# A local transformer's layers: softmax over whole PSUM banks, feed-forward parts and norm rows moved in the step

## The chip, the core and the metric

One core of a Trainium2 chip runs one launch. The metric is device time in microseconds. The core has a matmul engine (PE, with its weight loads shown as PEld), a vector engine (DVE), an activation engine (ACT), GpSimd (POOL), and SyncE (SP), which issues the DMAs. The engines take their instructions in program order, each from its own queue, and wait for each other by semaphores. [...]

## What is computed

The kernel runs two modulated layers over 16 sequences of 256 tokens and 128 channels. The change lies in the feed-forward part of the first, which is itself a local transformer of six layers (16 heads of 64, windows of 32 tokens):

```python
def attn_layer(x, Wqkv, qs, ksc, Wo):
    q, k, v = heads of x @ Wqkv
    q = l2norm(q) * qs
    k = l2norm(k) * ksc
    q = q * cos * scale + rotate_half(q) * sin * scale
    k = k * cos / scale + rotate_half(k) * sin / scale
    # each window of 32 queries sees its own 32 keys and the 32 before them
    sim = einsum('bhwie,bhwje->bhwij', bq, bk2) * 8
    sim = where(mask, -max, sim)
    attn = softmax(sim, -1)
    return heads joined (attn @ bv2) @ Wo

def ffn_layer(x, g, bln, W1, b1, W2, b2):
    mu = x.mean(-1); var = ((x - mu) ** 2).mean(-1)
    xn = (x - mu) / sqrt(var + 1e-05) * g + bln
    a, gate = split(xn @ W1 + b1)
    return a * gelu(gate) @ W2 + b2

for i in range(6):
    x = attn_layer(shift_tokens(x), ...) + x
    x = ffn_layer(shift_tokens(x), ...) + x
```

The output is (16, 256, 128), all in float32.

## The kernel before

Before the six layers stands a linear-attention stage, after them a multi-query attention stage; the change touches neither. The six layers run as one loop of steps `n` (line 1050), with the order on PE, DVE, ACT and POOL written out by hand: each engine runs its instructions in the order in which the program issues them.

A unit `u` is two sequences side by side, 512 columns; there are eight units and eight head pairs, and a step works on two head pairs of one unit, `m = 2n` and `2n + 1`. So a unit takes four steps, a layer 32, all six 192. A step is a software pipeline: it projects the head pairs of step n, adds the rotated halves for n - 1, fetches norm factors for n - 3, does scores and softmax for n - 4, flips the probabilities of n - 5, and so on. In program order a step issues:

- `scaled` (POOL): two products of keys with their norm factors `kn`, 128x512 each (line 795).
- `merging` (PE): 16 heads of the weighted state through the merged output weights into the `y` bank; at the end of a unit (n mod 4 = 0) `add_to_state` (DVE).
- in odd steps `norms_rows`: PE transposes the factors `rk`, ACT copies them, SP writes them to DRAM.
- place A: `go_on(behind)` lets the feed-forward of a finished unit, a generator, go on by one part; then the merging of the next layer's weights.
- `rotate` (POOL): four additions of the halves that came back by DMA (`got`).
- `flipped` for x = 0: four PE transposes of the probabilities `pr` and a copy to `prT` on ACT; then in odd steps `windows` (eight PE transposes, copies on ACT and DVE, a DMA); `masked`, which puts the mask into two `sim` banks by a bf16 matmul; `flipped` for x = 1, its copy on DVE.
- in even steps `norms_sum` (PE, 8 matmuls, a copy on ACT).
- `weighted`: 8 matmuls, and four copies to `zx` on ACT and DVE. Then place B.
- `scores`: 64 small matmuls into the two `sim` banks (par = 0 and 1, eight rows of 64 keys each). `maxima` (DVE): a maximum over keys for each bank, then `nb`, its product with the norm factors of the queries.
- in even steps `norms_inverse`: PE transposes, two DVE instructions (`nx`, `ny`), then 13 small POOL instructions, three rounds of an inverse square root. Then place C.
- `project`, twice (with place D after the first): for q and k a matmul, a square on ACT, two products on DVE; then four DMAs that swap halves (`got <- sent`). Between them `exponentials` is fed in, two at a time: 16 activations of 128x64, each with its own bias, scale and accumulated sum, `pr` straight from the `sim` banks.
- `divided`, once for each x: a reciprocal on DVE, and a product on POOL (line 880).
- `widened`: SP fetches `kn` from DRAM, four DMAs.

PSUM is divided into four rotating banks (`mm`), three for `sim` and one for `y`. An `mm` bank is written again when whoever read it four allocations before is done.

The feed-forward, appended to `behind` ahead of place C of a step with n mod 4 = 0, takes these places before the change: mean and its subtraction in C, the square in D; in the next step (n mod 4 = 1) variance, `rs` and `ex` (POOL, lines 972 and 974) in A, the transposes `rb` with the normalisation and the affine (line 981, DVE) in C; the gates with their GELU in A of the step after (2), `pa` in A of step 3, `py` in A of the next step 0.

Of the kernel before, what the change touches and what calls it, by code (L numbers as in the profile page):

```python
# [44 lines left out]
def adaln_kernel(  # L45
# [554 lines left out]
    with ExitStack() as es:  # L600
# [196 lines left out]
        def windows(u, s):  # L797


            xw = atile("xw", (128, 8, 128))  # L800
            for g in range(2):
                pt = bank()
                for j in range(4):
                    w0 = 32 * (4 * g + j)
                    nc.tensor.transpose(  # L805
                        pt[0:64, j * 128 : (j + 1) * 128], zs[u][:, s, w0 : w0 + 64], ident
                    )
                dst = xw[0:64, 4 * g : 4 * g + 4, :].rearrange("p w d -> p (w d)")
                if g:
                    nc.vector.tensor_copy(dst, pt[0:64, :])  # L810
                else:
                    nc.scalar.copy(dst, pt[0:64, :])
            nc.sync.dma_start(xw[64:128], xw[0:64])
            return xw
# [37 lines left out]
        def maxima(sim, rn):  # L852

            mx = small("mx", (128, 8))
            nc.vector.tensor_reduce(mx, sim.rearrange("p (b k) -> p b k", b=8), AX.X, ALU.max)  # L855
            nb = small("nb", (128, 8))
            nc.vector.scalar_tensor_tensor(nb, mx, -1.0, rn, ALU.mult, ALU.mult)  # L857
            return nb

        def exponentials(x, sims, nbs, rn, pr, ssum):  # L860

            for par in range(2):
                for st in range(4):
                    b = 4 * x + st
                    nc.scalar.activation(  # L865
                        pr[:, x, st, par, :],
                        sims[par][:, b * 64 : (b + 1) * 64],
                        AF.Exp,
                        bias=nbs[par][:, b : b + 1],
                        scale=rn[:, par, b : b + 1],  # L870
                        accum_out=ssum[:, x, st, par : par + 1],
                    )
                    if st % 2:
                        yield

        def divided(pr, ssum):
            rsum = small("rsum", (128, 8))
            nc.vector.reciprocal(rsum, ssum.rearrange("p t h -> p (t h)"))  # L878
            prf = pr.rearrange("p t h k -> p (t h) k")
            nc.gpsimd.tensor_tensor(  # L880
                prf, prf, rsum.unsqueeze(2).to_broadcast([128, 8, 64]), ALU.mult
            )

        def flipped(p, x, pr, prT):

            pt = bank()
            for st in range(4):
                nc.tensor.transpose(  # L888
                    pt[:, st * 128 : (st + 1) * 128],
                    pr[:, x, st].rearrange("p h k -> p (h k)"),  # L890
                    ident,
                )
            if x:
                nc.vector.tensor_copy(prT[:, p + x, :], pt)
            else:
                nc.scalar.copy(prT[:, p + x, :], pt)
# [51 lines left out]
        def ffn(u, i):  # L948
# [10 lines left out]
            yield  # L959
            pv = bank()  # L960
# [15 lines left out]
            yield  # L976
# [4 lines left out]
            nc.vector.tensor_scalar(xn, xn, bcol(i, "g"), bcol(i, "b"), ALU.mult, ALU.add)  # L981
            yield
            yield
# [9 lines left out]
            yield  # L993
            yield
            yield
            yield
# [9 lines left out]
            yield  # L1006
            yield
            yield
            yield
# [40 lines left out]
        while n < N + 9 or behind:  # L1050
# [26 lines left out]
            for s, lag in ((0, 7), (1, 9)):  # L1077
                v, r = divmod(n - lag, QS)
                if r == 0 and 0 <= v < DEPTH * NU:
                    xws[v, s] = windows(v % NU, s)  # L1080
            sims = masked() if 0 <= n - 4 < N else None
            if 0 <= n - 5 < N:
                flipped(p, 1, prs.pop(n - 5), prTs[i, u])

# [3 lines left out]
            if 0 <= v < DEPTH * NU:  # L1088
                zxs[v, r] = weighted(r, xws[v, r // 2], prTs[v // NU, v % NU])
            go_on(behind)  # L1090
            if sims:
# [4 lines left out]
                nbs = [maxima(sims[par], rn[:, par]) for par in range(2)]  # L1096
                ssum = small("ssum", (128, 2, 4, 2))
# [13 lines left out]
            if sims:  # L1111
                for x in range(2):
                    for _ in between:
                        pass
                    divided(pr[:, x], ssum[:, x])
                    between = exponentials(1, sims, nbs, rn, pr, ssum) if x == 0 else iter(())
# [481 lines left out]
```

## Time and profile before

| what | us |
|---|---|
| three runs: median (lowest to highest) | 4207.4 (4207.33 to 4213.38) |
| the profiled execution | 4207.77 |
| its span, first to last instruction | 4206.0 |
| first scores (line 843) to last ones in it | 303.0 to 3571.9 |
| busy in the span: PE, DVE, ACT, POOL | 3938.9, 2856.0, 2753.1, 2655.1 |

| row (line, engine, what) | count | mean ns |
|---|---|---|
| 865 ACT, one exponential of 128x64 | 3072 | 454 |
| 865 ACT, reading its accumulator | 3072 | 255 |
| 855 DVE, maximum of a bank | 384 | 685 |
| 857 DVE, `nb` 128x8 | 384 | 412 |
| 878 DVE, reciprocal 128x8 | 384 | 197 |
| 880 POOL, division of 128x512 | 384 | 1042 |
| 714 POOL, rotation, two full inputs | 768 | 1272 and 1292 |
| 795 POOL, keys times their factors | 384 | 1274 |
| 894 DVE and 896 ACT, copy to `prT` | 192 and 192 | 691 and 585 |
| 810 DVE and 812 ACT, copy of windows | 96 and 96 | 683 and 578 |
| 981 DVE, affine of the feed-forward | 48 | 835 |

Durations overlap where an engine starts the next instruction before the last one is out: eight exponentials in a row start 0.38 us apart although a row says 454 ns and each has a read of its accumulator behind it. In what follows a line of the timeline gives the start, the duration, the engine, the source line, the operation, output and inputs, the shapes, and in brackets how long the engine had been idle and what ended it. A line of the waits gives the engine, the line that waited, what it waited for, the sum in us, how often, and the longest.

### The profile page before, as it was taken

Reading aid. Unit: us, or ns where it says so; the run is one execution under the profiler, and the core shown is the slowest. Engines: PE = TensorE matmul, PEld = TensorE weight load, DVE = VectorE, ACT = ScalarE, POOL = GpSimd, SP = SyncE. Lnnn points to the kernel's source line nnn. Section 1 sums busy time; section 2 is a strip of 40 time slices with the busy share of each in tenths; the row PEclk is TensorE's granted clock in tenths of the full one; section 3 lists DMA queues with packets and bytes.
Section 4 is the critical chain, followed back from the end, with each engine's and each line's share of the span. In section 5 each row is a group of like instructions: output and inputs, shape, how many; then the busy total and the mean of one; then the engine's idle time right before and its main releaser. Section 6 shows DMA issues by size and latency. Waiting matters only on the chain.

```text
span 4206.0 us, 118202 instructions
## 1 busy us (share of the span) xinstructions
PE 3938.9 (94%) x45491; PEld 2580.1 (61%) x45491; DVE 2856.0 (68%) x6005; ACT 2753.1 (65%) x9640; POOL 2655.1 (63%) x3374
## 2 busy tenths in 40 slices
PE   7877999999999999999999999999999999799998
PEld 4534666666666666666666666666666666455554
DVE  6746767677767767676777777776767675476664
ACT  4535666667666666667666667666666766276665
POOL 5446666776666676666676766767666665155453
PEclk9878999999999999999999999999999999899999
DMA  1333444444444444444444444444434442200000
GB/s 41 41 90 97 106 109 105 109 107 105 106 105 114 104 110 105 105 110 102 111 109 105 112 103 106 108 110 105 110 100 105 104 105 72 64 1 6 9 3 11
DMA packets 193547, 371.06 MB, mean 88 GB/s; under 512 B 42537, under 2 KB 83416, under 8 KB 192984
## 3 DMA queue, kind: packets, MB, share of 16 engines
q1 hardware_dynamic: 192984, 363.50, 34.3%
q8 instruction: 360, 5.90, 0.6%
q14 instruction: 203, 1.66, 0.1%
HBM read 127.92 MB, written 8.91 MB: 33 GB/s over the span
## 4 chain that ended last, share of the span: by engine, by line
PE 46%; DVE 22%; ACT 19%; issue 7%; POOL 5%; DMA 1%; SPq 0%; POOLq 0%; DVEq 0%; ACTq 0%
ACT pr L865 11%; PE mm L906 9%; PE sim L843 7%; DVE sent L703 6%; ACT sq L701 4%; PE mm L722 4%; PE mm L888 4%; POOL pr L880 4%; DVE k L706 3%; DVE q L706 3%; PE mm L698 3%; DVE mx L855 3%; PE mm L805 2%; PE mm L1376 2%; PE sim L1303 2%
## 5 line engine op out<-in xcount | busy, mean ns | idle before, releaser
L865 ACT ACTIVATE pr<-sim,nb,rq 128x64 f32<-128x64 f32 x3072 | 1229.5, 454 | 336.8 <-DVE nb L857 318.3
L880 POOL TENSOR_TENSOR pr<-pr,rsum 128x512 f32<-128x512 f32 x384 | 398.3, 1042 | 807.3 <-DVE rsum L878 761.8
L865 ACT ACTIVATION_READ_ACCUMULATOR pr<-sim,nb,rq 128x1 f32 x3072 | 784.5, 255 | 0.0
L927 PEld LDWEIGHTS y<-zx,wvo 128*128 128x128 f32 x6144 | 716.1, 192 | 92.1 <-issue 89.0
L927 PE MATMUL y<-zx,wvo 128*128 128x128 f32 x6144 | 717.7, 275 | 1.3 <-ACT zx L921 1.2
L698 PE MATMUL mm<-z,wqk 128*128 128x512 f32 x1536 | 706.9, 602 | 8.6 <-DMA wqk<-in_L_ffn_Wqkv_dram 6.7
L703 DVE SCALAR_TENSOR_TENSOR sent<-mm,vec,rope 128x512 f32<-128x512 f32 x768 | 570.4, 743 | 118.2 <-ACT sq L701 110.2
L714 POOL TENSOR_TENSOR q<-q,got 128x512 f32<-128x512 f32 x384 | 488.3, 1272 | 12.7 <-DMA got<-sent 10.2
L714 POOL TENSOR_TENSOR k<-k,got 128x512 f32<-128x512 f32 x384 | 496.2, 1292 | 0.0
L795 POOL TENSOR_TENSOR k<-k,kn 128x512 f32<-128x512 f32 x384 | 481.9, 1274 | 17.9 <-DMA kn<-rkh 17.9
L701 ACT ACTIVATE sq<-mm 128x512 f32<-128x512 f32 x768 | 475.7, 619 | 23.3 <-PE mm L698 23.3
L698 PEld LDWEIGHTS mm<-z,wqk 128*128 128x128 f32 x1536 | 278.7, 192 | 322.9 <-issue 234.7
L919 DVE COPY zx<-mm 128x512 f32<-128x512 f32 x384 | 265.6, 692 | 262.0 <-PE mm L906 262.0
L921 ACT COPY zx<-mm 128x512 f32<-128x512 f32 x384 | 224.9, 586 | 287.0 <-PE mm L906 287.0
L906 PE MATMUL mm<-prT,xw 64*128 64x256 f32 x3072 | 389.7, 391 | 3.8 <-DVE zx L919 2.0
L855 DVE TENSOR_REDUCE mx<-sim 128x8 f32<-128x512 f32 x384 | 263.1, 685 | 171.9 <-PE sim L843 171.9
L906 PEld LDWEIGHTS mm<-prT,xw 64*128 64x128 f32 x3072 | 293.5, 187 | 121.7 <-issue 92.2
L1346 POOL TENSOR_TENSOR pr<-pr,rsum 128x256 f32<-128x256 f32 (+1 forms) x256 | 205.1, 832 | 241.7 <-DVE rsum L1344 218.3
L888 PE MATMUL mm<-ident,pr 128*128 128x128 f32 x1536 | 244.6, 282 | 105.1 <-POOL pr L880 75.9
L888 PEld LDWEIGHTS mm<-ident,pr 128*128 128x128 f32 x1536 | 174.9, 142 | 270.0 <-POOL pr L880 240.6
L843 PEld LDWEIGHTS sim<-k,q 64*32 64x32 f32 x24576 | 265.8, 105 | 83.3 <-issue 55.2
L843 PE MATMUL sim<-k,q 64*32 64x64 f32 x24576 | 299.7, 226 | 15.9 <-POOL k L795 8.1
(253 smaller groups left out, 6461.5 us busy)
## 6 DMA issues: line engine op xcount, KB each, us to landing
got<-sent SPq DMA_DIRECT2D x1536, 128.0 KB
kn<-rkh SPq DMA_DIRECT2D x768, 128.0 KB
xw<-xw SPq DMA_DIRECT2D x96, 256.0 KB
wqk<-in_L_ffn_Wqkv_dram SPq DMA_DIRECT2D x48, 128.0 KB
bhome<-brow SPq DMA_DIRECT2D x1, 3072.0 KB
wv<-in_L_ffn_Wqkv_dram SPq DMA_DIRECT2D x12, 256.0 KB
wo<-in_L_ffn_Wo_dram SPq DMA_DIRECT2D x12, 256.0 KB
xt<-in_x_dram SPq DMA_DIRECT2D x8, 256.0 KB
```

The source lines that it names most:

```text
L698: nc.tensor.matmul(pp, wqk[:, j, :], xs, start=True, stop=True)
L701: nc.scalar.activation(sq, pp, AF.Square)
L703: nc.vector.scalar_tensor_tensor(two(sent[:, j, :]), two(pp), scale, tab[1], ALU.mult, ALU.mult)
L714: nc.gpsimd.tensor_tensor(r, r, two(got[:, j, :]), ALU.add)
L795: nc.gpsimd.tensor_tensor(k, k, two(kn), ALU.mult)
L843: nc.tensor.matmul(sims[par][32 * c : 32 * c + 32, c0 : c0 + 64], q[r, s, t0 : t0 + 32], k[r, s, t0 : t0 + 64], start=False, stop=True, sk ...
L855: nc.vector.tensor_reduce(mx, sim.rearrange("p (b k) -> p b k", b=8), AX.X, ALU.max)
L865: nc.scalar.activation(pr[:, x, st, par, :], sims[par][:, b * 64 : (b + 1) * 64], AF.Exp, bias=nbs[par][:, b : b + 1], scale=rn[:, par, b ...
L880: nc.gpsimd.tensor_tensor(prf, prf, rsum.unsqueeze(2).to_broadcast([128, 8, 64]), ALU.mult)
L888: nc.tensor.transpose(pt[:, st * 128 : (st + 1) * 128], pr[:, x, st].rearrange("p h k -> p (h k)"), ident,)
L906: nc.tensor.matmul(pz[par][:, w * 256 : (w + 1) * 256], xw[r, (2 * k + w) % 8, :], prT[r, :, 64 * k + 32 * w : 64 * k + 32 * w + 32], star ...
L927: nc.tensor.matmul(py[:, j * 128 : (j + 1) * 128], vo[:, h, :], zx[:, h % 2, h // 2, :], start=(h == 0), stop=(h == 2 * NP - 1), skip_grou ...
```

## The change

The softmax is done a bank at a time. Instead of the maxima times the norm factors as a bias, and 16 activations with sums of their own, DVE subtracts the maximum from a bank of scores (into `pr`), POOL multiplies by the norm factor of the query, ACT takes one exponential over the bank, in place, DVE adds up over keys, and after one reciprocal POOL divides. The order of the generator puts exponentials, sums, reciprocal and both divisions behind the matmul of the third projection (q of the second head pair), that is ahead of the third and fourth squares on ACT and the last four products on DVE.

```diff
-        def maxima(sim, rn):
-            mx = small("mx", (128, 8))
-            nc.vector.tensor_reduce(mx, sim.rearrange("p (b k) -> p b k", b=8), AX.X, ALU.max)
-            nb = small("nb", (128, 8))
-            nc.vector.scalar_tensor_tensor(nb, mx, -1.0, rn, ALU.mult, ALU.mult)
-            return nb
...
+        def bank_of(pr, par):
+            return pr[:, :, :, par, :].rearrange("p x s k -> p (x s) k")
+
+        def over_keys(v):
+            return v.unsqueeze(2).to_broadcast([128, 8, 64])
+
+        def logits(sim, rn, dst):
+            sim = sim.rearrange("p (b k) -> p b k", b=8)
             mx = small("mx", (128, 8))
+            nc.vector.tensor_reduce(mx, sim, AX.X, ALU.max)
+            nc.vector.tensor_tensor(dst, sim, over_keys(mx), ALU.subtract)
+            nc.gpsimd.tensor_tensor(dst, dst, over_keys(rn), ALU.mult)
+
+        def softmaxed(pr):
+            yield
+            yield
             for par in range(2):
+                nc.scalar.activation(bank_of(pr, par), bank_of(pr, par), AF.Exp)
+            ssum = small("ssum", (128, 2, 4, 2))
+            for par in range(2):
+                nc.vector.tensor_reduce(
+                    ssum[:, :, :, par].rearrange("p x s -> p (x s)"), bank_of(pr, par), AX.X, ALU.add
+                )
+            rsum = small("rsum", (128, 16))
+            nc.vector.reciprocal(rsum, ssum.rearrange("p x t h -> p (x t h)"))
+            for x in range(2):
+                prf = pr[:, x].rearrange("p t h k -> p (t h) k")
+                nc.gpsimd.tensor_tensor(
+                    prf, prf, over_keys(rsum[:, 8 * x : 8 * x + 8]), ALU.mult
+                )
+            yield
```

Three copies or affines go from DVE to ACT: the second copies of `windows` and of `flipped`, and the affine of the feed-forward:

```diff
-            if x:
-                nc.vector.tensor_copy(prT[:, p + x, :], pt)
-            else:
-                nc.scalar.copy(prT[:, p + x, :], pt)
+            nc.scalar.copy(prT[:, p + x, :], pt)
...
-            nc.vector.tensor_scalar(xn, xn, bcol(i, "g"), bcol(i, "b"), ALU.mult, ALU.add)
+            nc.scalar.activation(xn, xn, AF.Identity, bias=bcol(i, "b"), scale=bcol(i, "g"))
```

In the loop the order becomes: `windows` ahead of the flips; in odd steps `masked` ahead of both flips, in even steps between them as before; `norms_rows` behind the flips; and the feed-forward is appended ahead of place B:

```diff
-            if n % 2 and 3 <= n <= N + 1:
-                home = norms_rows(rk)
             go_on(behind)
             go_on(merges)
...
+            for s, lag in ((0, 7), (1, 9)):
+                v, r = divmod(n - lag, QS)
+                if r == 0 and 0 <= v < DEPTH * NU:
+                    xws[v, s] = windows(v % NU, s)
             if 0 <= n - 5 < N:
...
+                if n % 2:
+                    sims = masked()
                 flipped(p, 0, prs[n - 5], prTs[i, u])
...
+            if n % 2 == 0 or n - 5 < 0:
+                sims = masked() if 0 <= n - 4 < N else None
             if 0 <= n - 5 < N:
                 flipped(p, 1, prs.pop(n - 5), prTs[i, u])
+            if n % 2 and 3 <= n <= N + 1:
+                home = norms_rows(rk)
...
+            if 0 <= w < DEPTH * NU and j == QS - 1:
+                behind.append(ffn(w % NU, w // NU))
             go_on(behind)
             if sims:
...
-                nbs = [maxima(sims[par], rn[:, par]) for par in range(2)]
-                ssum = small("ssum", (128, 2, 4, 2))
+                for par in range(2):
+                    logits(sims[par], rn[:, par], bank_of(pr, par))
...
-            if 0 <= w < DEPTH * NU and j == QS - 1:
-                behind.append(ffn(w % NU, w // NU))
             go_on(behind)
-            between = exponentials(0, sims, nbs, rn, pr, ssum) if sims else iter(())
+            between = softmaxed(pr) if sims else iter(())
```

The `yield`s between the parts of the feed-forward are counted anew, one more behind the square, one less behind `ex`, then three, five and three. Its places become: mean and subtraction in B of step 0, the square in C; variance, `rs` and `ex` in A of step 1 as before, `rb`, normalisation and affine in B; the gates in A of step 2 as before; `pa` in B of step 3; `py` in A of step 0 as before.

More of the change, by code (lines that the diff above doesn't have):

```diff
@@ L808, in windows @@
                 dst = xw[0:64, 4 * g : 4 * g + 4, :].rearrange("p w d -> p (w d)")
-                if g:
-                    nc.vector.tensor_copy(dst, pt[0:64, :])
-                else:
-                    nc.scalar.copy(dst, pt[0:64, :])
+                nc.scalar.copy(dst, pt[0:64, :])
             nc.sync.dma_start(xw[64:128], xw[0:64])
@@ L850, in scores @@
                             )
-        def maxima(sim, rn):
-            mx = small("mx", (128, 8))
-            nc.vector.tensor_reduce(mx, sim.rearrange("p (b k) -> p b k", b=8), AX.X, ALU.max)
-            nb = small("nb", (128, 8))
-            nc.vector.scalar_tensor_tensor(nb, mx, -1.0, rn, ALU.mult, ALU.mult)
-            return nb
-        def exponentials(x, sims, nbs, rn, pr, ssum):
-            for par in range(2):
[L863 to L882, printed above, removed]
+        def bank_of(pr, par):
+            return pr[:, :, :, par, :].rearrange("p x s k -> p (x s) k")
+        def over_keys(v):
+            return v.unsqueeze(2).to_broadcast([128, 8, 64])
@@ L892, in flipped @@
                 )
-            if x:
-                nc.vector.tensor_copy(prT[:, p + x, :], pt)
-            else:
-                nc.scalar.copy(prT[:, p + x, :], pt)
+            nc.scalar.copy(prT[:, p + x, :], pt)
         def weighted(j, xw, prT):
@@ L959, in ffn @@
             yield
+            yield
             pv = bank()
@@ L975, in ffn @@
             yield
-            yield
             rb = bank()
@@ L980, in ffn @@
             nc.vector.tensor_tensor(xn, xn, rb, ALU.mult)
-            nc.vector.tensor_scalar(xn, xn, bcol(i, "g"), bcol(i, "b"), ALU.mult, ALU.add)
-            yield
-            yield
+            nc.scalar.activation(xn, xn, AF.Identity, bias=bcol(i, "b"), scale=bcol(i, "g"))
+            for _ in range(3):
+                yield
             w1, w2 = wffs[i]
@@ L992, in ffn @@
                 gates.append(gt)
[L993 to L996, printed above, removed]
+            for _ in range(5):
+                yield
             for c, n in enumerate(FFC):
@@ L1005, in ffn @@
                 )
[L1006 to L1009, printed above, removed]
+            for _ in range(3):
+                yield
             py = bank()
@@ L1075, in adaln_kernel @@
                     prTs[i, u] = atile("prT", (128, NP, 512))
+                if n % 2:
+                    sims = masked()
                 flipped(p, 0, prs[n - 5], prTs[i, u])
[L1077 to L1081, printed above, removed]
+            if n % 2 == 0 or n - 5 < 0:
+                sims = masked() if 0 <= n - 4 < N else None
             if 0 <= n - 5 < N:
                 flipped(p, 1, prs.pop(n - 5), prTs[i, u])
+            if n % 2 and 3 <= n <= N + 1:
+                home = norms_rows(rk)
             if n % 2 == 0 and 2 <= n <= N:
@@ L1111, in adaln_kernel @@
             if sims:
[L1112 to L1116, printed above, removed]
+                for _ in between:
+                    pass
                 prs[n - 4] = pr
```

## The prediction

> **What bounds the kernel now.** I read the page's busy shares first, then the busy time by stretches, the waits, and last the timeline of four steps.
>
> ```profile
> PE 3938.9 (94%) x45491; PEld 2580.1 (61%) x45491; DVE 2856.0 (68%) x6005; ACT 2753.1 (65%) x9640; POOL 2655.1 (63%) x3374
> ```
> ```profile
> 1140.00:1660.00 520.00, 502.29 (x6573) 339.00 (x6574) 365.10 (x648) 359.04 (x1279) 358.84 (x456) 1.00 0.42 107
> ```
>
> The second line (length, then PE, PEld, DVE, ACT, POOL, clock, DMA share, GB/s) is a stretch in the middle of the layers. PE is busy 96.6% of it, the others about 70%, at clock 1.00. So PE sets the time, and a gain can only come from its gaps. What ends them:
>
> ```profile
> PEld mm L888 <- POOL pr L880: 240.6, 303, 7.5
> PE mm L888 <- POOL pr L880: 75.9, 126, 6.7
> POOL pr L880 <- DVE rsum L878: 761.8, 286, 8.9
> ACT pr L865 <- DVE nb L857: 318.3, 137, 5.9
> ```
>
> PE's flips wait for the division, and the division for the sums that come out of the 16 exponentials. The timeline gives the size:
>
> ```profile
> 1509.54 0.66 PE L740 MATMUL mm<-ident,n 128*128 128x128 f32 x4
> 1509.63 0.69 DVE L855 TENSOR_REDUCE mx<-sim 128x8 f32<-128x512 f32 x1 [0.67 <-PE sim L843]
> ...
> 1512.24 0.32 POOL L758 TENSOR_TENSOR na<-nx,ny 128x64 f32<-128x64 f32 x1 [1.27 <-DVE ny L751]
> ...
> 1516.65 0.26 POOL L766 TENSOR_TENSOR rq<-ny,na 128x32 f32<-128x32 f32 x1
> ...
> 1519.43 1.04 POOL L880 TENSOR_TENSOR pr<-pr,rsum 128x512 f32<-128x512 f32 x1 [2.53 <-DVE rsum L878]
> ...
> 1520.80 0.63 PE L888 MATMUL mm<-ident,pr 128*128 128x128 f32 x4 [0.44 <-ACT rkT L776]
> ```
>
> I call the moment when PE leaves the scores S (here 1509.54, a step with n mod 4 = 2), the flips of x = 0 and 1 flip0 and flip1, and the two divisions div0 and div1. POOL's norm chain ran from 1512.24 to 1516.91 (4.67 us) inside the exponentials; div0 ended at S + 10.93, flip0 started at S + 11.26: the last 0.3 went to a PSUM bank that the copy of the norm rows held on ACT, behind the exponentials.
>
> **PE without gaps.** From start to start in the timeline where nothing is waited for: a flip 0.50, mask 0.43, windows 0.88, norms_sum 1.86, weighted 1.92, scores 1.42 (1.51 in odd steps), norms_inverse 0.49, four projections 3.47, merging 3.57, rows 0.11; feed-forward: mean 0.86, variance 0.87, rb 0.49, gates, pa and py 2.58 each. A cycle of four steps (48 of them) adds up to 64.0 us. From flip0 at 1486.35 to the same flip at 1553.96 it took 67.6: 3.6 us of gaps, 173 us over the run. That is the most there is to gain.
>
> **The change, queue by queue.**
>
> ACT: 16 exponentials, 0.38 us from start to start where no square stands between (1517.37, 1517.75, 1518.13), 6.1 us a step, become two of 128x512. Nearest rows: L701 619 ns, L958 (SBUF to SBUF) 646 ns; I take 0.6, and in the walk below either end is covered. It gains a copy of prT (L896 585 ns), one of windows in odd steps and the feed-forward's affine; ACT's busy time should fall by 3072 x 0.38 = 1167 us and rise by some 440, to about 2020. The added copies cost nothing because ACT has 6 us a step less to do; without that cover each would be 0.58 us ahead of weighted.
>
> DVE: two subtractions are added (PSUM and SBUF in: L980 675 ns; not below it, and at most L703's 743) and two sums over keys (L458, a reduction from SBUF, 686 ns); the two nb (412 ns mean), a copy of prT, one of windows and L981 go. 265 + 262 - 158 - 133 - 66 - 40 - 37 (half of the reciprocals) = +93 us.
>
> POOL: two more multiplications a step, in place, with a broadcast second input. L880 is that form: 1042 ns, 1.03 apart. L714 with two full inputs takes 1272; that is my upper end, and L880's own time the lower, because nothing shorter of 512 elements but a copy (L974, 610 ns) is in the trace. I take L880's: +400 us, POOL to 3055.
>
> [...]
>
> **Walk of an even step** (S = 0; DVE instructions 0.66 apart, hand-over to POOL 0.16 as from rsum at 1519.27 to 1519.43). First maximum 0.09 to 0.78, subtraction to 1.5, second maximum to 2.2, subtraction to 2.9. POOL: first multiplication 1.66, second 3.06 to 4.1, then the norm chain, which the program puts there: 4.09 + 4.67 = 8.76. ACT: exponentials done by 4.8, or 5.4 behind a table load of 1.28. DVE: nx and ny, four projections' products to 5.9, sums to 7.3, reciprocal 7.5. So the sums are no longer last: **the norm chain is.** div0 8.76 to 9.80, div1 to 10.83.
>
> **Odd step:** no norm chain. Products to 5.5, sums to 6.85, reciprocal 7.1, div0 7.25 to 8.3, div1 to 9.33. If POOL comes 2.9 late (below), the second multiplication ends at 5.1, exponential 5.8, still ahead of the sums. A slack of 1.2 remains.
>
> The new wait of the exponentials for POOL holds up what is behind them on ACT, two squares, and so DVE's last four products, which wait for the squares and now for the sums too. The got transfers of the second head pair leave at S + 9.2 (odd) or 9.6 instead of 9.0; POOL wants them 5 or 6 us later, behind scaled and two rotations, and has 2 us in hand there before its multiplications. A landing time is not in the trace, only that two got transfers were ever waited for (10.2 us): nothing.
>
> PE's arrival at flip0 (steps named by n mod 4), and what ends the wait (banks of the four-deep pool are released by the products of the second head pair, now behind the sums: the last at 9.8 in odd, 10.3 in even steps):
> - into 1 (from 0): 0.49 + 3.47 + 3.57 + 0.87 + 0.88 + 0.43 = 9.71; flip1 could start at 10.21 but needs div1: 10.88. Lost 0.67.
> - into 2: 3.47 + 3.57 + 2.58 = 9.62; last bank 9.9. Lost 0.28.
> - into 3 (from 2): pa is now behind weighted, so 8.84; flip1 at 10.88 instead of 9.34. Lost 1.54.
> - into 0: 9.62; div0 at 8.3, nothing; 0.1 for small bank waits in all.
>
> And rb in step 1, moved ahead of the scores. Before, it came just in time:
>
> ```profile
> 1487.89 2.49 POOL L795 TENSOR_TENSOR k<-k,kn 128x512 f32<-128x512 f32 x2
> 1490.35 1.01 POOL L972 TENSOR_TENSOR rs<-ve,half 128x4 f32<-128x4 f32 x1
> 1491.42 0.61 POOL L974 COPY fs<-rs 128x512 f32<-128x512 f32 x1
> 1492.12 0.66 PE L979 MATMUL mm<-ident,fs 128*128 128x128 f32 x4
> ```
>
> From the end of div1 POOL needs 2.46 + 1.07 + 0.61 = 4.14 until ex is there. PE from flip1 to rb now has only 0.50 + 0.11 + 1.92 = 2.53. PE waits 1.6, with the scores queued behind it; POOL's four rotations (4.95) follow ex, so its multiplications start 2.9 after S there, which the odd step's slack takes.
>
> Moves that I cost at nothing: norms_rows behind the flips (0.11 PE, a 0.24 ACT copy, one DMA of rows on SP; the kn reads that need it are issued about 10 us later, behind the eight got transfers; with that gone L795 would start a transfer late); the mask ahead of the flips in odd steps (its sim banks are free at S + 2.9 instead of with the last exponential); mean ahead of the scores (its bank comes free before the maxima); the two nb, whose place the subtractions have taken in the walk.
>
> **Sum.** 64.0 + 0.67 + 1.6 + 0.28 + 1.54 + 0.1 = 68.2 us against 67.6: +0.6 a cycle, +29 us in 48. The last steps have no projections, and there the 16 exponentials set the pace (3555 to 3584 us): some 1.2 us less in each of four, -5. The profiled execution took 4207.8 (span 4206.0 and 1.8 around it), 0.4 above the median of 4207.4. 4207.4 + 29 - 5 = 4231.
>
> **Rivals.**
> - *Faster: POOL's norm chain is shorter than I walk it.* Its rows add up to (92.2 + 92.1 + 70.0 + 61.4 + 24.2 + 24.7) / 96 = 3.80 us a call; 0.87 of the 4.67 are gaps between dependent instructions. For it: everything in even steps hangs on this one chain. Against it: the gaps stood beside an idle queue. At 3.80 div1 ends at 9.96; step 1 loses 0.6 to its bank, rb 0.8, step 3 (bank again) 1.0, the rest 0.4: 66.8 a cycle, -0.8, so 4207 - 38 - 5 = 4164. It turns a loss into a gain from 0.3 us on; any other 0.5 us off the even step does the same. With all gaps gone, the floor is 4207 - 173 = 4034.
> - *Slower still: the multiplications cost what L714 does.* +0.23 twice in an even step, 0.46 on flip1 in steps 1 and 3: +0.92 a cycle, 4275. For it: the written rows are strided, unlike L880's. Against it: the broadcast input is the same.
> - *An even trade:* the moved feed-forward parts save the small bank waits ("PEld mm L698 <- DVE fx L980" and such) that I count on neither side, 0.5 a cycle, and the total stays at 4207.
> - *It doesn't do what it says* would be a bank-wide exponential near 16 small ones in price; L701's 619 ns excludes it.
>
> **How the numbers follow.** Forecast 45% (own range 4212 to 4255), shorter chain 31%, dearer multiplications 14%, even trade 10%. 0.2% (8.4 us) is about what a measurement can tell from no change. Slower: 0.41 of the forecast and all of the dearer ones, 0.55. Same: 0.03 of the forecast, 0.01 of the shorter chain, 0.08 of the trade, 0.12. Faster: 0.30 of the shorter chain, 0.01 and 0.02 of the forecast and the trade, 0.33. The range, 4155 to 4295, reaches a little beyond the times of both rivals, and leaves out what lies further on.
>
> **What would show it.** Right: PE waits at rb for ex, about 48 x 1.6 = 75 us; flip1 of an odd step starts just behind div1, with no POOL gap between the second multiplication, the norm chain and the divisions; ACT near 2020 us busy, POOL near 3050, PE's unchanged at 3939. Wrong: rb without a wait, or a POOL gap ahead of the divisions in even steps (then the sums are still last), or PE busy above 97.5% in the middle stretch.

## The result and the profile after

The changed kernel takes 4424.3 us (median of four runs, 4416.95 to 4425.93) against 4207.6 before: ratio 1.051, 95% interval 1.049 to 1.053. It is slower, as forecast, but by 217 us instead of 24, outside the range. The profiled execution, the shortest of the four, took 4417.0, its span 4414.8. First the busy shares on its page, then the same middle stretch as before (columns as there):

```profile
PE 3999.6 (91%) x45491; PEld 2614.5 (59%) x45491; DVE 3035.9 (69%) x5861; ACT 2054.7 (47%) x4216; POOL 3032.3 (69%) x3758
```
```profile
1140.00:1660.00 520.00, 482.08 (x6147) 324.07 (x6150) 370.30 (x586) 233.76 (x394) 387.80 (x479) 0.98 0.41 101
```

ACT and POOL came out as costed (2054.7 against some 2020; 3032 against 3055). PE fell from 96.6% to 92.7% of the stretch, and two things are new in it: PE's own busy time over the run rose by 60.7 us for the same 45491 matmuls, and the granted clock is 0.98 instead of 1.00. The waits say what PE lacks:

```profile
POOL k L795 <- DMA kn<-rkh: 276.4, 51, 9.1
POOL pr L879 <- DVE rsum L876: 261.3, 97, 3.1
ACT pr L869 <- POOL pr L862: 208.3, 316, 6.3
PE mm L888 <- POOL pr L879: 133.5, 94, 5.2
PE sim L840 <- POOL k L795: 72.1, 51, 7.2
PE mm L976 <- POOL fs L972: 51.7, 45, 2.0
```

Line 879 is the division (880 before), 869 the exponential, 840 the scores (843), 976 rb (979). The division's wait for the sums fell from 761.8 to 261.3, as the walk has it. The first line is the surprise: POOL waits 276 us for `kn`, 51 times 5.4 us, where it waited 17.9 in all before; and the scores wait for POOL's `k`. The timeline shows one such place (SPq is SP's queue; steps n mod 4 = 1 and 2):

```profile
2014.08 1.40 SPq L786 DMA_DIRECT2D kn<-rkh  x2
2020.16 0.54 SPq L708 DMA_DIRECT2D got<-sent  x1
...
2026.14 0.59 SPq L709 DMA_DIRECT2D got<-sent  x1
2026.77 6.59 SPq L786 DMA_DIRECT2D kn<-rkh  x6
...
2030.67 1.26 POOL L795 TENSOR_TENSOR k<-k,kn 128x512 f32<-128x512 f32 x1 [5.01 <-DMA kn<-rkh]
...
2031.98 0.86 PE L840 MATMUL sim<-k,q 64*32 64x64 f32 x64 [1.04 <-POOL k L795]
2032.77 0.66 PE L740 MATMUL mm<-ident,n 128*128 128x128 f32 x4
...
2036.79 2.04 POOL L862 TENSOR_TENSOR pr<-pr,rq 128x512 f32<-128x512 f32 x2
...
2043.42 2.04 POOL L879 TENSOR_TENSOR pr<-pr,rsum 128x512 f32<-128x512 f32 x2
...
2044.52 0.66 PE L888 MATMUL mm<-ident,pr 128*128 128x128 f32 x4 [2.59 <-POOL pr L879]
```

SP issues two of the four `kn` reads at 2014.08, stands still from 2015.5 to 2020.2 until DVE's products are there to be swapped (over the run SP waits 1363 us at L708 for DVE's L703), issues the eight got transfers, and only then, 12.7 us behind the first, the reads for the second head pair (the next four with them). POOL idles 5.01 us for them. PE loses 1.04 in the scores, and POOL's four rotations and two multiplications come behind: the first multiplication starts at S + 4.02 (S = 2032.77) instead of the walk's 1.66, the divisions at S + 10.65 instead of 8.76, and the flip waits 2.59. Before, SP issued all four reads in one go, 8.8 us ahead of the next got:

```profile
1489.27 2.49 SPq L786 DMA_DIRECT2D kn<-rkh  x4
1498.04 0.55 SPq L708 DMA_DIRECT2D got<-sent  x1
```

SP's order isn't among the four that are written out by hand (PE, DVE, ACT, POOL), and it isn't the program's, which has the reads of a step behind its got transfers; what places it no run shows. Counting the instructions on SP between writes of `rkh`, the kernel before has four reads ahead of the eight got transfers in 91 pairs of steps; the changed one has two in 46 of them (the steps n mod 4 = 1), and six behind.

### The profile page after: what moved, and what is told of

It reads as the page before. It is cut to its first block, busy times and chain, and to the rows that moved or that the text cites. A ratio compares the mean times of both kernels' runs of the same rounds, so it can differ in the third digit from the quotient of the medians.

```text
span 4414.8 us, 113394 instructions
## 1 busy us (share of the span) xinstructions
PE 3999.6 (91%) x45491; PEld 2614.5 (59%) x45491; DVE 3035.9 (69%) x5861; ACT 2054.7 (47%) x4216; POOL 3032.3 (69%) x3758
## 4 chain that ended last, share of the span: by engine, by line
PE 45%; DVE 19%; POOL 15%; issue 8%; DMA 6%; SPq 4%; ACT 2%; POOLq 0%; DVEq 0%; ACTq 0%
PE mm L903 5%; PE mm L698 5%; PE y L924 5%; PE sim L840 5%; POOL pr L879 4%; DMA kn<-rkh 4%; DVE sent L703 4%; PE mm L994 3%; DVE mx L860 3%; DVE pr L861 3%; PE mm L888 2%; PE mm L1005 2%; DVE ssum L872 2%; PE mm L722 2%; PE mm L1369 2%
## 5 line engine op out<-in xcount | busy, mean ns | idle before, releaser
L698 PE MATMUL mm<-z,wqk 128*128 128x512 f32 x1536 | 726.4, 613 | 8.9 <-DMA wqk<-in_L_ffn_Wqkv_dram 6.8
L701 ACT ACTIVATE sq<-mm 128x512 f32<-128x512 f32 x768 | 435.0, 591 | 618.1 <-PE mm L698 618.1
L795 POOL TENSOR_TENSOR k<-k,kn 128x512 f32<-128x512 f32 x384 | 482.6, 1273 | 276.5 <-DMA kn<-rkh 276.4
L703 DVE SCALAR_TENSOR_TENSOR sent<-mm,vec,rope 128x512 f32<-128x512 f32 x768 | 571.2, 744 | 13.7 <-ACT sq L701 11.3
L879 POOL TENSOR_TENSOR pr<-pr,rsum 128x512 f32<-128x512 f32 x384 | 392.6, 1044 | 261.3 <-DVE rsum L876 261.3
L862 POOL TENSOR_TENSOR pr<-pr,rq 128x512 f32<-128x512 f32 x384 | 397.0, 1045 | 242.8 <-DVE pr L861 242.7
L903 PE MATMUL mm<-prT,xw 64*128 64x256 f32 x3072 | 416.2, 408 | 2.6 <-DVE zx L916 2.0
L893 ACT COPY prT<-mm 128x512 f32<-128x512 f32 x384 | 221.6, 585 | 410.1 <-PE mm L888 403.4
L903 PEld LDWEIGHTS mm<-prT,xw 64*128 64x128 f32 x3072 | 310.5, 197 | 131.0 <-issue 101.8
L888 PE MATMUL mm<-ident,pr 128*128 128x128 f32 x1536 | 247.7, 290 | 139.1 <-POOL pr L879 133.5
L840 PE MATMUL sim<-k,q 64*32 64x64 f32 x24576 | 305.5, 228 | 74.8 <-POOL k L795 72.1
L888 PEld LDWEIGHTS mm<-ident,pr 128*128 128x128 f32 x1536 | 188.5, 147 | 259.9 <-POOL pr L879 199.0
L869 ACT ACTIVATE pr<-pr 128x512 f32<-128x512 f32 x384 | 240.8, 631 | 208.8 <-POOL pr L862 208.3
```

What stands on the lines that cost most here:

```text
L698: nc.tensor.matmul(pp, wqk[:, j, :], xs, start=True, stop=True)
L701: nc.scalar.activation(sq, pp, AF.Square)
L703: nc.vector.scalar_tensor_tensor(two(sent[:, j, :]), two(pp), scale, tab[1], ALU.mult, ALU.mult)
L795: nc.gpsimd.tensor_tensor(k, k, two(kn), ALU.mult)
L840: nc.tensor.matmul(sims[par][32 * c : 32 * c + 32, c0 : c0 + 64], q[r, s, t0 : t0 + 32], k[r, s, t0 : t0 + 64], start=False, stop=True, sk ...
L862: nc.gpsimd.tensor_tensor(dst, dst, over_keys(rn), ALU.mult)
```

## Experiments: the late reads

My theory after the result, L: the reads that slipped behind the got transfers are the whole excess, and without them the walk stands. The rivals: P, the bank softmax itself (POOL's longer queue) costs it; and R, the norm rows cost by their new place on PE and ACT.

**The reads in front again.** The changed kernel, with the `kn` reads issued right behind the norm rows:

```diff
             if n % 2 and 3 <= n <= N + 1:
                 home = norms_rows(rk)
+            if 0 <= n - 3 < N:
+                for m in (2 * (n - 3), 2 * (n - 3) + 1):
+                    kns[m] = widened(m, home)
...
-            if 0 <= n - 3 < N:
-                for m in (2 * (n - 3), 2 * (n - 3) + 1):
-                    kns[m] = widened(m, home)
```

> The changed kernel, with the four kn reads issued in program order right behind the norm rows instead of at the end of the step; in SP's queue all four then stand ahead of the eight got transfers in every pair of steps (in the changed kernel, in half of the pairs two of the four stand behind them). Theory L (the late kn reads are the cause): POOL's 276 us of waits for kn go, PE's waits for the second half of the keys go, and the time falls to what the walk had without them, 4231, say 4200 to 4270. Theory P (POOL's own load, multiplications and norm chain, is the cause, the waits for kn are only slack): 4380 to 4425. Theory R (norm rows behind the flips cost by their place on PE and ACT): no change, 4400 to 4425.

Measured: 4217.0, ratio 1.0019 (1.001 to 1.0029). 207 of the 217 us are gone with nothing else changed, which neither P (4380 to 4425) nor R (4400 to 4425) allows. SP's queue and PE's waits in it:

```profile
2039.56 0.67 SPq L778 DMA_DIRECT2D rkh<-rkT  x1
2042.07 2.94 SPq L786 DMA_DIRECT2D kn<-rkh  x4
2048.14 0.54 SPq L708 DMA_DIRECT2D got<-sent  x1
```
```profile
PE mm L888 <- POOL pr L879: 72.4, 101, 5.0
PE mm L976 <- POOL fs L972: 45.8, 41, 2.0
PE mm L805 <- ACT xw L809: 27.5, 41, 0.7
...
POOL k L795 <- DMA kn<-rkh: 6.5, 6, 4.5
PE sim L840 <- POOL k L795: 3.3, 3, 2.8
```

All four reads stand ahead, and POOL waits 6.5 us for them in all. The two spans differ by 192.3 us, and the rows account for it: PE's waits at the scores 72.1 - 3.3 = 68.8, at the flips 133.5 - 72.4 = 61.1, at rb 5.9, and PE's busy time 3999.6 - 3945.4 = 54.2 (most of it the clock, below): 190.0. From here on this kernel is "the mended one".

**The same reads in the kernel before**, as a control, since early reads might help any kernel.

> The kernel before, with the kn reads issued behind the second flip, as in the kernel that mended the changed one. A control: theory L (early kn reads help only where they had slipped behind the got transfers) says that the time is that before, 4203 to 4213, since they stand ahead of them there already. Rival G (kn reads early are a gain in any kernel, so that they hid a loss elsewhere in the changed one): 4100 to 4190.

Measured: 4201.2, ratio 0.9979 (0.9969 to 0.9988): 2 us below L's range, 11 above G's. The cycles from rb to rb are 67.6 us as before; some 5 us go in the first steps, ahead of the first rb. So early reads gain some 9 us here (0.2%), and the mended kernel's 207 us are not a general gain.

**Norm rows in front again.** The changed kernel, with `norms_rows` back ahead of place A; everything else as changed.

```diff
+            if n % 2 and 3 <= n <= N + 1:
+                home = norms_rows(rk)
             go_on(behind)
...
                 flipped(p, 1, prs.pop(n - 5), prTs[i, u])
-            if n % 2 and 3 <= n <= N + 1:
-                home = norms_rows(rk)
```

> The changed kernel with the norm rows back at their old place, ahead of place A; kn reads at the end of the step as in both kernels. SP's queue has four kn reads ahead of the got transfers in nearly all pairs again. Theory L: 4200 to 4290, as e1. Theory P: 4380 to 4425. Theory R: 4200 to 4290 here, but not in e1.

Measured: 4281.5, ratio 1.0166 (1.0151 to 1.0182). Better than the changed kernel by 143 us, worse than the mended one by 65. L and R forecast the same range here, and it holds; the run with the reads in front, where R forecast no change, tells them apart. Its waits:

```profile
PEld mm L774 <- POOL rk L765: 129.9, 96, 6.0
PE mm L774 <- POOL rk L765: 109.8, 96, 5.1
...
POOL k L795 <- DMA kn<-rkh: 53.6, 11, 6.6
```

With the bank softmax the norm chain runs behind both multiplications, so `rk` is ready later, and PE, which reaches the transposes of the rows (L774) first, waits for it in each of the 96 odd steps. The old place has a price of its own in the new softmax; the new place has one only through SP's queue.

**The old softmax with the norm rows behind the flips**, and **the new softmax alone in the kernel before**:

```diff
-            if n % 2 and 3 <= n <= N + 1:
-                home = norms_rows(rk)
             go_on(behind)
...
                 flipped(p, 1, prs.pop(n - 5), prTs[i, u])
+            if n % 2 and 3 <= n <= N + 1:
+                home = norms_rows(rk)
```
```diff
-                nbs = [maxima(sims[par], rn[:, par]) for par in range(2)]
-                ssum = small("ssum", (128, 2, 4, 2))
+                for par in range(2):
+                    logits(sims[par], rn[:, par], bank_of(pr, par))
...
-            between = exponentials(0, sims, nbs, rn, pr, ssum) if sims else iter(())
+            between = softmaxed(pr) if sims else iter(())
```

> The kernel before with one edit, the norm rows behind the flips. In SP's queue three kn reads now stand ahead of the got transfers and one behind, in nearly all pairs of steps. Theory L: half of the second head pair's factors arrive about 8 us later, POOL waits for kn some 3 to 6 us in half of the steps; POOL has some 4 us of idle time a step there, so the loss is between nothing and the 217 us of the whole change, most likely 60 to 200 us: 4270 to 4400. Theory P: 4200 to 4220, since POOL's load is unchanged. Theory R: 4210 to 4240, 0.4 us of PE and ACT work at another place.

> The kernel before with the softmax by whole banks alone: copies, feed-forward, windows, mask and norm rows stay where they were. SP's queue as before. Theory L: no wait for kn; the norm chain on POOL ends the even steps 0.1 us sooner than the exponentials did, the odd steps 1 us sooner, pa stays ahead of the flips: 4150 to 4230. Theory P: most of the loss is here, 4330 to 4425. Theory R: 4150 to 4230.

Measured: 4233.9, ratio 1.0059 (1.0042 to 1.0075), and 4258.6, ratio 1.0117 (1.0102 to 1.0132). The first lies in R's range (4210 to 4240), not in the one that I held most likely for L (4270 to 4400); the second lies in nobody's. In the first, one of the four reads stands behind the got transfers in most pairs of steps, and POOL waits for reads 92 times, 1.5 us each; the whole move costs 26 us:

```profile
POOL pr L880 <- DVE rsum L878: 727.5, 279, 10.3
...
POOL k L795 <- DMA kn<-rkh: 135.9, 92, 8.9
PE mm L888 <- POOL pr L880: 114.7, 131, 6.6
```

I read it so: with the old softmax POOL idles 727.5 us for the sums, and a late multiplication of keys mostly moves that idle time; the new softmax has POOL work there, and the lateness goes on to PE. PE's wait at the flips grew by 38.8 us here for 135.9 us of POOL's waits, and in the changed kernel by 61.1 against the mended one, with 68.8 more at the scores, for 276.4. That is argued and not shown apart: here fewer reads are late, and PE has a new wait of 28.4 us for a copy to `prT` at L805, so the reads' own share of the 26 us stays open. In the second kernel PE waits 53.2 us for `rk` at L774 (and its weight load 69.2), the wait of the kernel with the rows in front. So by these waits the new softmax asks for the later norm rows, and the later norm rows need the reads kept in front of the got transfers.

## Experiments: the walk

The mended kernel is what I had walked; I forecast a cycle of 68.2 us. From rb to rb it takes 68.3 (most of 47 cycles lie between 68.25 and 68.5, a few at layer ends up to 73.8; before 67.6 and up to 71.7). One of its even steps (S = 2059.55):

```profile
2059.55 0.66 PE L740 MATMUL mm<-ident,n 128*128 128x128 f32 x4
2062.52 1.04 POOL L862 TENSOR_TENSOR pr<-pr,rq 128x512 f32<-128x512 f32 x1 [0.21 <-DVE pr L861]
2062.61 1.00 DVE L751 TENSOR_SCALAR ny<-nx 128x64 int32<-128x64 int32 x1
2068.11 0.26 POOL L766 TENSOR_TENSOR rq<-ny,na 128x32 f32<-128x32 f32 x1
2068.33 2.04 POOL L879 TENSOR_TENSOR pr<-pr,rsum 128x512 f32<-128x512 f32 x2
```

The rest tests single terms.

**Three rounds to two.** The mended kernel with two of the three rounds of the inverse square root in `norms_inverse`: four POOL instructions fewer in the norm chain. The norm factors are less exact.

```diff
-            for it in range(3):
+            for it in range(1, 3):
```

> e1 with two of the three rounds of the inverse square root left out to one less: the norms get two rounds instead of three, so POOL's norm chain is four instructions, some 1.45 us, shorter; nothing else changes. Walk W (the norm chain ends the even steps): flip1 of the odd steps comes 1.1 us sooner, until the sums or a bank are last, 4100 to 4170. Rival S (the sums are last in even steps, the norm chain stands in their shadow): 4210 to 4225.

Measured: 4175.9, ratio 0.992 (0.9906 to 0.9933); cycles of 67.4. That is 6 us above W's range and 34 below S's.

```profile
POOL pr L879 <- DVE rsum L876: 357.9, 190, 3.1
PE mm L888 <- POOL pr L879: 49.2, 94, 4.9
```

In the mended kernel the chain ends the even steps, as walked: without four of its instructions PE's wait at the flips falls from 72.4 to 49.2 and at rb from 45.8 to 28.7. Of the 3.0 us taken out in a cycle's two chains only 0.9 come through, for POOL now waits some 1.0 us for the reciprocal ahead of the divisions of each even step (190 waits instead of 97): the sums are last again, having been some 0.6 ahead of the longer chain.

**rb behind the scores again**, in place C, in the mended kernel:

```diff
             nc.gpsimd.tensor_copy(ex, rs.unsqueeze(2).to_broadcast([128, 4, 128]))
             yield
+            yield
             rb = bank()
...
-            for _ in range(3):
+            for _ in range(2):
                 yield
```

> e1 (kn reads early) with rb and the normalisation back in place C, behind the scores. Walk W (PE waits there for ex because rb was moved ahead of the scores): the wait of some 1.1 us in each of 48 cycles goes, 4155 to 4190. Rival B (PE is held at the next place by the same amount, by a bank or by the flips): 4205 to 4225.

Measured: 4234.6, ratio 1.0059 (1.0046 to 1.0071): 18 us slower than the mended kernel, not faster, and above the ranges of both W and B. The wait at rb is gone, but PE pays twice for it:

```profile
2051.80 1.12 PE L698 MATMUL mm<-z,wqk 128*128 128x512 f32 x2 [0.32 <-DVE fx L978]
...
2058.82 1.06 PE L987 MATMUL mm<-fx,w 128*85 128x512 f32 x2 [0.60 <-DVE q L706]
```

rb's product on DVE now stands behind both maxima and subtractions (2051.07), so a bank comes free late for the projections, DVE's products are late, and the gates wait for the last of their banks. Placing rb ahead of the scores was right even at a wait of some 1.1 us a cycle.

**nx and ny ahead of the scores**, in the mended kernel: `norms_inverse` ends with `ny`, and its POOL chain, now the generator `norms_rounds`, keeps its place:

```diff
             for it in range(3):
+                if it == 2:
+                    yield
...
+            if n % 2 == 0 and 2 <= n <= N:
+                xy = norms_inverse(n2)
             if sims:
                 m = 2 * (n - 4)
...
             if n % 2 == 0 and 2 <= n <= N:
-                rk, inverses[n // 2 - 1] = norms_inverse(n2)
+                done = []
+                rounds = norms_rounds(*xy, done)
+                next(rounds)
+                for _ in rounds:
+                    pass
+                rk, inverses[n // 2 - 1] = done
```

> e1 with the transposes of norms_inverse and its two DVE instructions ahead of the scores, so that they don't stand behind the subtractions; the POOL rounds stay behind the multiplications. In e1, ny takes 1.0 us there instead of 0.2 while POOL multiplies, and the bank of the transposes is late for the fourth projection (62 us of weight loads waiting for nx). Walk W: 4175 to 4210. Rival (these waits are covered): 4213 to 4225, or slower if the transposes delay the scores.

Measured: 4293.0, ratio 1.0197 (1.0183 to 1.0211), 76 us slower than the mended kernel, cycles of 69.7: far above W's range, and a much larger loss than the rival's.

```profile
2026.08 0.66 PE L740 MATMUL mm<-ident,n 128*128 128x128 f32 x4
2026.66 1.48 PE L846 MATMUL sim<-k,q 64*32 64x64 f32 x128
2026.83 0.21 DVE L742 TENSOR_SCALAR nx<-mm 128x64 f32<-128x64 f32 x1
2027.08 0.89 DVE L751 TENSOR_SCALAR ny<-nx 128x64 int32<-128x64 int32 x1
...
2029.80 1.04 POOL L868 TENSOR_TENSOR pr<-pr,rq 128x512 f32<-128x512 f32 x1 [1.89 <-DVE pr L867]
...
2036.69 2.04 POOL L885 TENSOR_TENSOR pr<-pr,rsum 128x512 f32<-128x512 f32 x2
2037.79 0.66 PE L894 MATMUL mm<-ident,pr 128*128 128x128 f32 x4 [1.14 <-POOL pr L885]
```

`ny` is done at 2027.97, before the maxima, but the chain stays behind the multiplications on POOL. The divisions start at S + 8.62 (S = 2028.07), 0.16 earlier than in the mended kernel, whereas PE has lost the 0.49 us of transposes that lay between S and the flips: the wait grows. By this working that is 0.33 an even step, 0.7 of the 1.4 us a cycle; the rest I have not traced.

**ex ahead of the keys.** The mended kernel, with `scaled` behind the feed-forward's part in place A, so that POOL makes `rs` and `ex` before it multiplies keys; and the same with two rounds, whose first has other constants so that two are enough (relative error 8e-7):

```diff
-            if 0 <= n - 4 < N:
-                for m in (2 * (n - 4), 2 * (n - 4) + 1):
-                    scaled(m, kns.pop(m))
...
             go_on(behind)
+            if 0 <= n - 4 < N:
+                for m in (2 * (n - 4), 2 * (n - 4) + 1):
+                    scaled(m, kns.pop(m))
             go_on(merges)
```
```diff
-                y.bitcast(I32), x.bitcast(I32), -0.5, float(0x5F3759DF), ALU.mult, ALU.add
+                y.bitcast(I32), x.bitcast(I32), -0.5, float(0x5F1FFFF9), ALU.mult, ALU.add
...
-            for it in range(3):
+            for it in range(2):
...
-                nc.gpsimd.tensor_scalar(a, a, -0.5, 1.5, ALU.mult, ALU.add)
-                if it < 2:
+                c = (-0.5, 1.5) if it else (-0.703952253, 1.68191391)
+                nc.gpsimd.tensor_scalar(a, a, c[0], c[1], ALU.mult, ALU.add)
+                if it < 1:
```

> The kernel with the early kn reads (4217 us), and in POOL's order rs and ex of the feed-forward (1.02 + 0.61 us) now stand ahead of the two multiplications of keys (2.5 us) instead of behind them. Theory Q (only POOL's queue makes rb late in step 1): ve is there 0.1 us after div1 (2037.07 against 2036.95), so ex is there at about 2038.75 and PE, which reaches rb at 2040.0, doesn't wait; the wait at rb falls from 46 us to under 5, a cycle from 68.35 to about 67.25 us, the total to 4155 to 4175. Rival K (the wait moves on to the scores): the keys are multiplied 1.6 us later, the scores wait for POOL's L795 as long as rb did, 40 us or more in all, and the total stays at 4205 to 4225.

> The one before, and the inverse square root in two rounds instead of three, with first-round constants (0x5F1FFFF9, 0.703952253, 1.68191391) for which two rounds give a relative error of 8e-7: four small POOL instructions, 1.5 us, less in each even step. Theory Q together with the chain as the end of even steps: the steps into 3 lose 0.8 us of waiting as they did in the run with two rounds (67.4 against 68.35 us a cycle, of which 0.43 was at rb and is gone already), so some 0.5 a cycle and 10 us in the first steps less than the kernel before it: 4115 to 4140. Rival K: the scores wait for the keys in both, and the total stays at 4165 to 4185, what two rounds alone gave. Rival V: with the chain shorter, ve (behind DVE's last four products) is what rs waits for and the first head pair's k comes late behind it: 4145 to 4165.

Measured: 4202.1, ratio 0.998 (0.9969 to 0.9992), cycles of 67.8; and 4179.0, ratio 0.9922 (0.9902 to 0.9941), cycles of 67.4. The first lies between Q and K:

```profile
2031.44 0.65 PE L976 MATMUL mm<-ident,fs 128*128 128x128 f32 x4
2032.03 1.69 PE L840 MATMUL sim<-k,q 64*32 64x64 f32 x128
...
2042.90 1.06 PE L986 MATMUL mm<-fx,w 128*85 128x512 f32 x2 [0.27 <-DVE q L706]
```

At rb PE no longer waits. Half of it comes back: the scores take 1.69 instead of 1.57, and the gates wait 0.27 for a bank that DVE's last products hold. That is the "0.28 into 2" of my walk, which the wait at rb had covered. With two rounds on top the time is K's, that of two rounds alone, but not by K's wait: PE waits 3.3 us for the keys at the scores in the whole run. Against two rounds alone its wait at rb falls from 28.7 to 2.0 and the one at the flips stays (49.4), but PE's busy time rises by 24.7 us, 9.6 of them in the scores. I have not traced the rest.

**Two more.** The windows' transposes ahead of the variance in place A (mended kernel, two rounds with those constants), to learn whose bank makes PE wait 0.67 at L805 in the step into 1:

```diff
+            for s, lag in ((0, 7), (1, 9)):
+                v, r = divmod(n - lag, QS)
+                if r == 0 and 0 <= v < DEPTH * NU:
+                    xws[v, s] = windows(v % NU, s)
             go_on(behind)
             go_on(merges)
...
-            for s, lag in ((0, 7), (1, 9)):
-                v, r = divmod(n - lag, QS)
-                if r == 0 and 0 <= v < DEPTH * NU:
-                    xws[v, s] = windows(v % NU, s)
```

> The kernel with the early kn reads and two rounds of inverse square root (with the first-round constants that make two enough; 4176 us with the plain ones), and in place A of step 1 the windows' transposes now stand ahead of the feed-forward's variance instead of behind it. Theory B (the second windows' bank is short there only because the variance holds one until DVE has read it, behind its products): the 0.67 us in which PE waits for ACT's copy in the step into 1 go, as they don't stand in the step into 3, a cycle from 67.4 to about 66.8 us, the total to 4135 to 4155. Rival A (two copies one behind the other on ACT, which before went to ACT and DVE, take that long in any place): the wait stays and the total is 4168 to 4185.

Measured: 4177.3, ratio 0.9919 (0.9902 to 0.9935): A's time, though not A's wait. The 0.67 is gone, but the variance waits 0.23 for the copy of windows, the rows' transpose 0.24 for the copy of prT, and rb's wait grew from 0.68 (two rounds alone) to 0.81: what was won at one bank is lost at the next places. And a combination (rb in C, nx ahead, the third round of the chain behind the divisions, the second head pair's rotations behind the multiplications in odd steps):

```diff
-                for m in (2 * (n - 1), 2 * (n - 1) + 1):
+                for m in (2 * (n - 1), 2 * (n - 1) + 1)[: 1 if n % 2 and sims_next(n) else 2]:
                     rotate(m, qs[m], got.pop(m))
...
                     logits(sims[par], rn[:, par], bank_of(pr, par))
+                if n % 2 and 2 * (n - 1) + 1 in got:
+                    rotate(2 * (n - 1) + 1, qs[2 * (n - 1) + 1], got.pop(2 * (n - 1) + 1))
...
                 prs[n - 4] = pr
+            if n % 2 == 0 and 2 <= n <= N:
+                for _ in rounds:
+                    pass
+                rk, inverses[n // 2 - 1] = done
```

> e5 and e7 together, and POOL reordered: in even steps the third round of the norms behind the divisions, in odd steps the rotation of the second head pair behind the multiplications. Walk W: flips of odd steps wait for the sums alone, rb not at all; some 2 to 3 us less in a cycle than e1: 4060 to 4130, ahead of the kernel before. Rival: the third round behind the divisions makes scaled and with it the scores late, 4150 to 4230.

Measured: 4211.3, ratio 1.0004 (0.9995 to 1.0013), where rb in C alone gave 4234.6 and nx ahead alone 4293.0. That is in the rival's range, but what PE waits for now is `rk` at the rows' transposes: 37.1 us in 50 waits, against 5.3 in the mended kernel. If the costs of the first two moves add up, the last two, or one of them, make up for them; neither was tried alone. No kernel's median is below 4175.9. Of those whose norm factors are good to 8e-7, the ones with the windows in front (4177.3) and with ex ahead (4179.0) are no different by their intervals, and both are quicker than the two kernels of this case by 0.7% or more.

## Why the prediction was wrong, point by point

- **The step that failed** is the first of the "moves that I cost at nothing": "norms_rows behind the flips (… the kn reads that need it are issued about 10 us later, behind the eight got transfers; with that gone L795 would start a transfer late)". I named the queue and the consequence, and then let it cost nothing without saying what hides it. The runs put 207 us on it. The delay itself was about right (12.7 us where shown, in every other pair of steps); what was wrong is that it costs nothing. POOL waited 276.4 us for the reads, 5.4 us each time, and PE behind it at the scores and the flips. That the change had just filled the POOL time in which such a lateness would have been lost is what the old softmax suggests (26 us for the same move of the rows), not a thing shown by itself.
- **The direction** was right by luck: 207 of the 217 us come from what I put at nothing, and the mended kernel is 0.2% slower than the one before, which is as much as I had said can be told from no change.
- **The sum without it**: 4231 forecast, 4217 in the mended kernel, inside the forecast's own range (4212 to 4255). The cycle is 68.2 forecast, 68.3 measured, partly by luck (the terms, below). The first steps, up to the first rb, gained 12 us that I had not looked at (463.6 to 451.3). The end from the last rb took 584.1 us in this execution against 578.1; the changed kernel took 578.3 there, so that I don't count it.
- **The walk of an even step** holds: divisions at S + 8.76 and 9.80 to 10.83 walked, S + 8.78 to 10.82 in the mended kernel (2068.33 to 2070.37, S = 2059.55), with no gap above 0.15 on POOL from the second multiplication to the end (lines above). The run with two rounds confirms that the chain is last here.
- **The terms** of the 4.2 us of gaps, taken from start to start: rb 1.6 walked, 1.29 found; into 3 1.54, 1.44 found; into 2 0.28, hidden behind rb and found as 0.27 once that was gone; into 1 0.67 at flip1, not there: the windows' second bank, which I had at nothing, took 0.83 just ahead and so hid the division. 3.56 in all. "PE without gaps" is then 68.35 - 3.56 = 64.8, not 64.0: projections take 3.54 instead of 3.47 from start to start, pa 2.77 instead of 2.58, the mean 1.05 instead of 0.86. So the cycle came out because 0.6 us too much of gaps and 0.8 too little of work nearly cancel.
- **What would show it**: rb waits, but 46 us (52 in the changed kernel) instead of 75; POOL without a gap in even steps, right. ACT's and POOL's busy times and a wait at rb showed in the changed kernel too, whose time I missed by 193 us: none of my signs looked at the reads. "PE's unchanged at 3939" holds for the mended kernel (3945.4), not for the changed one.
- **The rivals.** Shorter chain: excluded by the walk's S + 8.78. Dearer multiplications: line 862 takes 1045 ns, as line 880 did (1042), so the written stride costs nothing here. The even trade would be right for the mended kernel to within 0.2%, by compensation: 0.7 us a cycle lost, the first steps won. The 207 us belong to none of the rivals: none named the kn reads.
- **DVE** rose by 180 us instead of 93; 72.7 of the 87 in excess are `ny` alone (below).

## What to carry to other kernels

A step that is moved takes its DMAs along, and a queue that nobody ordered by hand may put them behind transfers that wait for something else (12.7 us behind the first two reads here); before costing that at nothing, look up what those wait for, and when the moved transfer's reader needs it. Where a change takes up an engine's idle time, a lateness that this idle time used to absorb may be uncovered: price both together, not each in the old kernel. And moving one wait of a chain that several waits share (rb, the flips, the banks) moved the next one into its place in three of the runs (rb behind the scores, ex and the windows ahead): 1.1 us at rb gave 0.5 a cycle.

## What the hardware showed that I had not expected

**A gap of PE, and a clock of 0.50 behind it.** The changed kernel's timeline at another cycle, and its windows there (the clock is the third number from the right):

```profile
1378.88 0.59 PE L818 MATMUL sim<-maskb,ident 128*128 128x512 bf16 x2
1382.05 2.11 PE L888 MATMUL mm<-ident,pr 128*128 128x128 f32 x8 [2.57 <-POOL pr L879]
...
1384.31 3.79 PE L903 MATMUL mm<-prT,xw 64*128 64x256 f32 x16
```
```profile
1376.00:1380.00 4.00, 3.48 (x30) 2.97 (x28) 3.97 (x8) 2.70 (x6) 3.27 (x11) 1.00 0.62 145
1380.00:1384.00 4.00, 1.95 (x9) 1.56 (x9) 1.20 (x2) 0.59 (x1) 3.83 (x7) 0.70 0.54 128
1384.00:1388.00 4.00, 4.00 (x18) 2.54 (x16) 0.69 (x1) 1.32 (x3) 4.00 (x5) 0.50 0.38 84
```

After a wait of 2.57 us the granted clock is 0.50; eight flips take 2.11 us instead of 1.12, the weighted state 3.79 instead of 2.00. Stretch by stretch of 1 us the clock is 0.80 from 1381, 0.50 from 1382 to 1388, 0.78 behind that and 1.00 from 1389: 6 us at 0.50 behind one gap. Behind the wait of 2.59 that ends at 2044.52 the clock stayed at 1.00 (2044 to 2058), so not every gap of this length is followed by it. What tells the two apart no run here shows. An estimate for the layers, PE's busy time times the clock that is missing, summed over stretches of 4 us, is 50 us in the changed kernel and 5 in the mended one: 45 of the 57 us that PE is busier there. The rest I have not traced.

**A small DVE instruction under POOL.** `ny` (128x64, one input, SBUF to SBUF) took 214 ns on average before and 971 in the changed kernel, where it meets POOL's multiplications or rotations; `nx`, which reads PSUM just ahead of it and meets them too, stayed at 215. In the mended kernel one `ny` ran from 2062.61 to 2063.61, and the multiplication on POOL from 2062.52 to 2063.56: it ends when POOL does. So do all in the changed kernel, 0.04 to 0.06 us behind an instruction of 128x512 on POOL; in the kernel before two met a rotation and took 1.08 us, and the others met nothing and took 0.2. Why `ny` lasts so long there and `nx` does not, no run here shows. With three rounds the step's end is not moved by it, since the chain stands behind that multiplication on POOL anyway; with two, the sums end the step, and I estimate from 996 ns a `ny` in that run and 214 before that they are 0.8 us later for `ny` ahead of them on DVE.
